# Expert weights loaded in two parts from two copied tables, in a two-layer decoder on one Trainium2 core

## The chip, the core and the metric

One core of a Trainium2 chip runs the whole program. The time is in device microseconds (us) for one execution; lower is better. The engines are PE (TensorE: matrix products and transposes; PEld is its weight load), DVE (VectorE), ACT (ScalarE), POOL (GpSimd) and SP (SyncE, which here only issues DMAs). Each engine works through its own instructions in a fixed order. Sixteen DMA engines are shared by all queues: q1 takes what SP issues, q0 what POOL issues, q10 what ACT issues.

## The reference

Sixteen blocks of 128 tokens, 512 wide, go through two decoder layers, each of self attention, cross attention and a feed-forward part, with a layernorm after each of the six. The first attention of layer 0, where a part of the change ends up, is

```
scores = einsum('btkgd,bskd->bkgts', qg, k) * scale + tril(ones)
p = softmax(scores, axis=-1)
out = einsum('bkgts,bskd->btkgd', p, v).reshape(B, T, C) @ wo.T + bo
```

The last part of layer 1, which the change is about, is a mixture of experts. A gate picks 2 of 8 experts for each of the 2048 tokens; each expert has a gate and an up weight (512 x 352 each) and a down weight (352 x 512), and a shared expert of twice that width serves all tokens:

```
logits = x @ gate_weight.T; scores = softmax(logits)
topk_w, topk_idx = top_k(scores, 2)
gu = einsum('th,efh->tef', x, gate_up_weights)
act = silu(gu[..., :F]) * gu[..., F:]
y = einsum('tef,te,ehf->th', act, combine, down_weights)
y += (silu(x @ sg.T) * (x @ su.T)) @ shared_down.T
```

All of it is in float32.

## The kernel before

**The stages** follow each other on PE nearly without a break: first attention (to about 260 us), cross attention of layer 0, its ternary feed-forward part (from about 743 us; called FFN below), linear attention, cross attention of layer 1, and the experts (from about 1489 us). A scheduler orders the instructions of each engine when the program is built. It keeps dependences and whatever is marked `keep_in_program_order`; anything else it may put elsewhere in its engine's queue.

**The first attention** works block by block. For each block and each of four groups of heads (a chunk, below), PE makes scores (L488), DVE adds the mask and takes the maximum (L212, L214), ACT takes the exponentials with their sums (L219), DVE the reciprocal of the sums (L225), and POOL scales the probabilities by it (`finish`, L226). One block later PE transposes the probabilities (`turn`, L231) and multiplies them with the values (L494). Beside this, the products of the next four blocks (L165) are dealt out between the chunks. POOL also prepares rotated weights (L377) and adds an output bias to the 16 blocks of x (L448, 1.26 us each). Between 12 and 61 us SP's queue brings in x, copies of x for later (`turned<-in_x`, L393, from DRAM to DRAM in pieces of 128 bytes), and two raw weight blocks of 1728 KB (L424).

**The experts.** The two choices of each token are ranked and sorted into 39 tiles of 128 token places (`NT`), each tile of one expert. For each tile a row list `which` tells which 128 rows of the weight array to fetch. A tile's weights (`ew`) are 128 partitions x 4352 floats, 2.23 MB: the first 2816 columns (`GU`) are gate and up, the last 1536 the down weights. There are three buffers for them (`HELD`). One indirect DMA, issued by POOL (`Tile.load`, L1241), fills a buffer from the input array `l1f_w`. Tile t uses buffer t modulo 3. Where tile t has the same expert as tile t - 3, the row numbers are set out of bounds and the DMA moves nothing, so an expert costs at most three real loads.

The loop over steps (from 1657 us on) is a pipeline. In step s: tile s is transposed by DVE (`turn`); `up` (L1271) makes gate and up of tile s - 1; `turn_act` (L1283) and `down` (L1292) finish tile s - 2; then a share of the shared expert's down products (L1326, L1334) follows on PE. The load for tile s + 1 is issued after the down products of tile s - 2, the last readers of that buffer. After it POOL issues the accumulating DMA that adds the tile's result to the DRAM array `sums` (L1304). That one waits for the accumulation before it, so POOL's queue in a step reads: load, accumulate. The token rows come through SP's queue in pieces of 512 bytes (`xs<-slots_x`, L1253).

After the last tile, `sums` is read back and the last layernorm ends the program (to 2057.5 us).

Of the kernel before, what the change touches and what calls it, by code (L numbers as in the profile page):

```python
# [12 lines left out]
F32 = mybir.dt.float32  # L13
# [33 lines left out]
def decoder_kernel(ctx: ExitStack, tc: tile.TileContext, a: dict, out: bass.AP):  # L47
# [669 lines left out]
    p2w.__exit__(None, None, None)  # L717
    psum.share(mm=2, sc=3, pt=2, av=1)

    wq4 = []
    with tc.tile_pool(name="p3", bufs=1) as p3:
        w1, w2 = (tern.w[n].rearrange("p (k f) -> p k f", k=KC) for n in range(2))
        def inputs(g):
            xh = p3.tile([P, KC, TG], F32R, tag="xh", name="xh", bufs=2)
            xl = p3.tile([P, KC, TG], F32R, tag="xl", name="xl", bufs=2)

            turns = [Turn(g * GB + i) for i in range(GB)]  # L730

            def sent(i):
                turns[i].send(p3)
                turns[i].fetch(p3, bufs=2)

            def one(i):
                at = slice(i * P, (i + 1) * P)
                if g == 0:
                    tr = bank(("mm", "sc")[i % 2], [P, KC, P], "tr")
                    for k in range(KC):  # L740
                        nc.tensor.transpose(tr[:, k, :], x[i][:, k * P : (k + 1) * P], ident)
                else:
                    tr = p3.tile([P, KC, P], F32, tag="xT", name="xT")
                    turns[i].back(tr)
                nc.scalar.copy(xh[:, :, at], tr)
                nc.vector.tensor_tensor(xl[:, :, at], tr, xh[:, :, at], ALU.subtract)

            if g == 0:
                return (xh, xl), [lambda i=i: one(i) for i in range(GB)]
            order = [(sent, 0), (sent, 1), (one, 0), (sent, 2), (one, 1), (sent, 3), (one, 2), (None, 0), (one, 3)]  # L750
            return (xh, xl), [lambda f=f, i=i: f and f(i) for f, i in order]

        xs, todo = inputs(0)
        for run in todo:
            run()
        todo = [lambda q=q: tern.cut(2, q, p3, tern.load(2, q, p3)) for q in range(NP)]
        todo.pop(0)()
        todo.pop(0)()
        for g in range(NG):
            hs = []  # L760
            if g + 1 < NG:
                coming, more = inputs(g + 1)
                todo += more
            for f in range(NF0):
                for _ in range(-(-len(todo) // (NF0 - f)) if f else 0):
                    todo.pop(0)()
                pa = bank("sc", [P, TG], "pa")
                pb = bank("pt", [P, TG], "pb")
                for dst, wt in ((pa, w1), (pb, w2)):
                    for k in range(KC):  # L770
                        for n in range(2):
                            nc.tensor.matmul(  # L772
                                dst, lhsT=wt[:, k, f * P : (f + 1) * P], rhs=xs[n][:, k, :],
                                start=(k == 0 and n == 0), stop=(k == KC - 1 and n == 1),
                            )
                sg = p3.tile([P, TG], F32, tag="sg", name="sg", bufs=2)
                nc.scalar.activation(sg, pa, AF.Sigmoid)
                ht = p3.tile([P, TG], F32, tag="ht", name="ht", bufs=2)
                nc.vector.tensor_tensor(ht, sg, pb, ALU.mult)
                hh = p3.tile([P, TG], F32R, tag="hh", name="hh", bufs=NF0 + 1)  # L780
                nc.scalar.copy(hh, ht)  # L781
                hl = p3.tile([P, TG], F32R, tag="hl", name="hl", bufs=NF0 + 1)
                nc.gpsimd.tensor_tensor(hl, ht, hh, ALU.subtract)  # L783
                hs.append((hh, hl))
            w3 = tern.w[2].rearrange("p (f d) -> p f d", d=D)
            if g + 1 < NG:
                xs = coming
            else:

                for n in range(2):  # L790
                    t = pre.tile([P, 2, 3 * D], F32, tag="pre", name=f"wq4{n}")
                    nc.sync.dma_start(t, a["l1a_wqkv"][:, 2 * n : 2 * n + 2, :])
                    wq4.append(t)
            for i in range(GB):
                b = g * GB + i
                po = bank("mm", [P, D], "po")
                for f in range(NF0):
                    for n in range(2):
                        nc.tensor.matmul(  # L799
                            po, lhsT=hs[f][n][:, i * P : (i + 1) * P], rhs=w3[:, f, :],  # L800
                            start=(f == 0 and n == 0), stop=(f == NF0 - 1 and n == 1),
                        )
                nc.vector.tensor_tensor(x[b], x[b], po, ALU.add)
                layernorm(b)
# [245 lines left out]

    GU = KC * 2 * FE
    with tc.tile_pool(name="p6", bufs=1, reuse_waits="tile") as p6:
        acts, halves = {}, {}
        w12 = []
# [167 lines left out]
                    ))  # L1224


        table = a["l1f_w"].rearrange("n p f -> (n p) f")
        with tc.tile_pool(name="p6r", bufs=1, side="right", reuse_waits="tile") as p6r:

            held = []  # L1230
# [1 line left out]
            class Tile:  # L1232
                def __init__(self, t):
                    self.t = t

                def load(self):
                    t = self.t
                    if t < HELD:
                        held.append(p6.tile([P, EW], F32, tag="ew", name=f"ew{t}", bufs=HELD))
                    self.w = held[t % HELD]  # L1240
                    tc.keep_in_program_order(nc.gpsimd.indirect_dma_start(  # L1241
                        out=self.w, out_offset=None, in_=table,
                        in_offset=bass.IndirectOffsetOnAxis(ap=which[:, t : t + 1], axis=0),
                        bounds_check=E * P - 1, oob_is_err=False,
                    ))
# [16 lines left out]
                        self.x.rearrange("p t (k a) -> p t k a", k=KC),  # L1262
                    ))

                def up(self):
                    gu = gate_up(self.w)
                    pg = bank("sc", [P, FE], "rg")
                    pu = bank("sc", [P, FE], "ru")
                    for dst, off in ((pg, 0), (pu, FE)):
                        for k in range(KC):  # L1270
                            nc.tensor.matmul(  # L1271
                                dst, lhsT=self.xT[:, k, :], rhs=gu[:, k, off : off + FE],
                                start=(k == 0), stop=(k == KC - 1),
                            )
                    sg = p6.tile([P, FE], F32, tag="sg", name="rsg", bufs=3)
                    nc.scalar.activation(sg, pg, AF.Silu)  # L1276
                    self.act = p6r.tile([P, FE], F32, tag="ract", name="ract", bufs=2)
                    nc.vector.tensor_tensor(self.act, sg, pu, ALU.mult)
# [9 lines left out]
                def down(self, following):  # L1288
                    dn = down_w(self.w)
                    po = bank("av", [P, D], "ry")  # L1290
                    for m_, mw in enumerate(ECH):
                        nc.tensor.matmul(  # L1292
                            po, lhsT=self.actT[:mw, m_, :], rhs=dn[:mw, m_, :], start=(m_ == 0), stop=(m_ == 2)
                        )
                    if following is not None:
                        following.load()
                    place = p6r.tile([P, 1], mybir.dt.int32, tag="place", name="place", bufs=3)
                    own = NC + NB + self.t
                    tc.keep_in_program_order(
                        nc.vector.tensor_tensor(place, self.told[:, 1:2], ramp[:, own : own + 1], ALU.add)  # L1300
                    )
                    y = p6.tile([P, D], F32, tag="y", name="ry", bufs=3)
                    nc.vector.tensor_scalar(y, po, self.told[:, 0:1], None, ALU.mult)
                    nc.gpsimd.indirect_dma_start(  # L1304
                        out=sums, out_offset=bass.IndirectOffsetOnAxis(ap=place, axis=0),
                        in_=y, in_offset=None, compute_op=ALU.add,
                    )
# [39 lines left out]
            for g in range(NG):  # L1347
                for n in range(2):
                    if (n, g) != (0, 0):
                        hidden(n, g, send)  # L1350
                if g != 2:
                    ahead[len(ahead)] = Tile(len(ahead))
                    ahead[len(ahead) - 1].load()
            for t in ahead.values():
                t.fetch()

# [5 lines left out]
            for step in range(NT + 2):  # L1362
# [5 lines left out]
                if step < NT:  # L1368
                    ahead[step].turn()
                if 0 <= step - 1 < NT:  # L1370
                    ahead[step - 1].up()
                if 0 <= step - 2:
                    ahead.pop(step - 2).down(ahead[step + 1] if step + 1 < NT else None)
                if step < NT:
# [189 lines left out]
```

## Time and profile before

| What | Time, us |
|---|---|
| runs of the kernel before | 2058.14, 2063.01, 2064.41 (median 2063.01) |
| the profiled execution, its own time | 2059.38 |
| its span, first to last instruction | 2057.5 |
| PE busy in the span | 2006.5 |
| POOL busy in the span | 647.5 |
| 39 weight loads on POOL (L1241), in all | 40.6 |
| 39 accumulating issues on POOL (L1304), in all | 61.8 |

The profile is of one execution. A "busy" time counts an engine's own instructions; the clock granted to PE was 0.992 of full speed over the span. In a row of the timeline the columns are start, duration, engine, line, operation, output<-inputs, shape and how many equal instructions were merged; a bracket at the end tells how long the engine was idle just before, and what ended that. In a row of the waits they are: who waited, for whom, microseconds in total, how many times, the longest. In a table by windows each row is one stretch of the span, with the busy time of each engine, the granted clock, the busy share of the DMA engines and the bytes they moved in GB/s.

### The profile page before, as it was taken

Reading aid. Unit: us, or ns where it says so; the run is one execution under the profiler, and the core shown is the slowest. Engines: PE = TensorE matmul, PEld = TensorE weight load, DVE = VectorE, ACT = ScalarE, POOL = GpSimd, SP = SyncE. Lnnn points to the kernel's source line nnn. Section 1 sums busy time; section 2 is a strip of 40 time slices with the busy share of each in tenths; the row PEclk is TensorE's granted clock in tenths of the full one; section 3 lists DMA queues with packets and bytes.
Section 4 is the critical chain, followed back from the end, with each engine's and each line's share of the span. In section 5 each row is a group of like instructions: output and inputs, shape, how many; then the busy total and the mean of one; then the engine's idle time right before and its main releaser. Section 6 shows DMA issues by size and latency. Waiting matters only on the chain.

```text
span 2057.5 us, 25359 instructions
## 1 busy us (share of the span) xinstructions
PE 2006.5 (98%) x9045; PEld 1110.9 (54%) x9045; DVE 886.6 (43%) x1775; ACT 627.7 (31%) x2107; POOL 647.5 (31%) x674
## 2 busy tenths in 40 slices
PE   8999999999999999999999999999899999999997
PEld 4555554444444468888554444555544455555552
DVE  4777732445554354342134414777731123233234
ACT  3555532333333333222311012766522200000002
POOL 7445520211222122223422113455613212323223
PEclk9999999999999999999999999999999999999999
DMA  9201241535432241001410018500013246786844
GB/s 250 87 17 40 104 143 56 158 118 174 149 124 91 71 121 60 16 11 62 147 42 21 11 41 265 203 22 22 27 61 116 95 133 185 226 247 192 264 89 169
DMA packets 164110, 227.87 MB, mean 111 GB/s; under 512 B 50576, under 2 KB 117520, under 8 KB 159248
## 3 DMA queue, kind: packets, MB, share of 16 engines
q1 hardware_dynamic: 149088, 152.80, 23.9%
q0 software_dynamic: 13792, 72.14, 11.6%
q8 instruction: 72, 1.18, 0.2%
q10 hardware_dynamic: 1104, 1.31, 0.2%
q14 instruction: 54, 0.44, 0.1%
HBM read 185.88 MB, written 75.83 MB: 127 GB/s over the span
## 4 chain that ended last, share of the span: by engine, by line
PE 84%; DMA 6%; DVE 3%; POOL 2%; issue 2%; ACT 1%; SPq 0%; POOLq 0%; DVEq 0%; ACTq 0%
PE po L649 10%; PE po L176 7%; PE pq L590 5%; PE pq L868 5%; PE pq L165 5%; PE pg L1143 4%; PE po L799 4%; PE pa L772 4%; PE pb L772 4%; PE pu L1143 3%; DMA sums<-ry,place 3%; PE ry L1292 3%; PE rg L1271 3%; PE ru L1271 3%; PE pv L878 3%; PE av L637 3%
## 5 line engine op out<-in xcount | busy, mean ns | idle before, releaser
L226 POOL TENSOR_TENSOR p<-p,rs 128x512 f32<-128x512 f32 x192 | 201.0, 1048 | 456.9 <-DVE rs L225 447.6
L649 PE MATMUL po<-mT,cc 128*128 128x512 f32 x512 | 230.4, 598 | 1.4 <-ACT cc L642 1.4
L219 ACT ACTIVATE p<-t,nmx 128x128 f32<-128x128 f32 x512 | 198.6, 390 | 33.8 <-POOL p L226 10.2
L649 PEld LDWEIGHTS po<-mT,cc 128*128 128x128 f32 x512 | 94.7, 190 | 115.0 <-issue 106.0
L219 ACT ACTIVATE p<-sc,nmx 128x128 f32<-128x128 f32 x256 | 90.3, 374 | 109.1 <-DVE nmx L214 93.8
L1241 POOL DMA_INDIRECT ew<-in_l1f_w_dram,which x39 | 40.6, 1042 | 246.6 <-PE ry L1292 167.2
L176 PE MATMUL po<-wo,oT 128*128 128x512 f32 x256 | 116.9, 600 | 0.4 <-ACT qkT L454 0.4
L590 PE MATMUL pq<-xT,wqr 128*128 128x512 f32 x256 | 115.8, 593 | 0.9 <-ACT xT L129 0.9
L1276 ACT ACTIVATE rsg<-rg 128x352 f32<-128x352 f32 x39 | 18.1, 464 | 320.6 <-PE rg L1271 297.0
L115 POOL TENSOR_SCALAR ve<-mv 128x1 f32<-128x1 f32 x80 | 17.8, 223 | 301.4 <-DVE mv L113 282.9
L868 PE MATMUL pq<-xT,wq 128*128 128x512 f32 x256 | 110.6, 592 | 0.7 <-ACT xT L129 0.7
L1292 PE MATMUL ry<-ew,ractT 128*128 128x512 f32 (+1 forms) x234 | 106.9, 592 | 0.0
L1271 PE MATMUL rg<-ew,xsT 128*128 128x352 f32 x312 | 100.1, 463 | 6.6 <-DMA ew<-in_l1f_w_dram,which 6.5
L122 POOL TENSOR_SCALAR x<-x,mv,rstd 128x512 f32<-128x512 f32 x48 | 100.5, 2094 | 4.5
L1271 PE MATMUL ru<-ew,xsT 128*128 128x352 f32 x312 | 98.7, 459 | 0.0
L219 ACT ACTIVATION_READ_ACCUMULATOR p<-t,nmx 128x1 f32 x512 | 96.3, 188 | 0.0
L233 DVE COPY pT<-pt 128x512 f32<-128x512 f32 x128 | 86.6, 679 | 19.4 <-PE pt L231 19.4
L783 POOL TENSOR_TENSOR hl<-ht,hh 128x512 fp32r<-128x512 f32 x44 | 57.4, 1305 | 108.1 <-ACT hh L781 108.1
L231 PEld LDWEIGHTS pt<-ident,p 128*128 128x128 f32 x512 | 60.6, 143 | 55.5 <-issue 41.5
L1143 PE MATMUL pg<-xT,sw_gu 128*128 128x512 f32 x192 | 86.5, 593 | 0.0
L1304 POOL DMA_INDIRECT sums<-ry,place x39 | 61.8, 1585 | 70.4 <-DMA sums<-ry,place 34.7
L214 DVE TENSOR_REDUCE nmx<-t 128x4 f32<-128x512 f32 x128 | 83.6, 676 | 0.8
(243 smaller groups left out, 3612.4 us busy)
## 6 DMA issues: line engine op xcount, KB each, us to landing
piece<-in_l0f_w_dram SPq DMA_DIRECT2D x48, 352.0 KB
away<-sq SPq DMA_DIRECT2D x32, 512.0 KB
pT<-away SPq DMA_DIRECT2D x128, 128.0 KB
raw<-in_l0x_raw_dram SPq DMA_DIRECT2D x8, 1728.0 KB
x<-turned SPq DMA_DIRECT2D x176, 64.0 KB
slots_x<-zero SPq DMA_DIRECT2D x1, 10023.0 KB
sums<-zero SPq DMA_DIRECT2D x1, 9984.0 KB
xs<-slots_x SPq DMA_DIRECT2D x156, 64.0 KB
```

Source lines behind the costliest of these rows:

```text
L122: engine.tensor_scalar(x[b], x[b], mean, rstd, ALU.subtract, ALU.mult)
L165: nc.tensor.matmul(got["p"], lhsT=lhsT, rhs=rhs, start=(n == 0), stop=(n == len(pairs) - 1))
L176: nc.tensor.matmul(po, lhsT=oT[:, c, :], rhs=wo[:, c, :], start=(c == 0), stop=(c == KC - 1))
L219: nc.scalar.activation(self.p[:, j, :], src[:, j, :], AF.Exp, bias=nmx[:, j : j + 1], accum_out=self.sm[:, j : j + 1])
L226: nc.gpsimd.tensor_tensor(self.p, self.p, spread(rs, P), ALU.mult)
L590: nc.tensor.matmul(pq, lhsT=wqr[:, k, cols], rhs=xT[:, k, :], start=(k == 0), stop=(k == KC - 1))
L649: nc.tensor.matmul(self.po, lhsT=self.cc[:, 4 * par + j, :], rhs=mT[h], start=(par == 0 and j == 0), stop=(par == 1 and j == 3),)
L772: nc.tensor.matmul(dst, lhsT=wt[:, k, f * P : (f + 1) * P], rhs=xs[n][:, k, :], start=(k == 0 and n == 0), stop=(k == KC - 1 and n == 1),)
L868: nc.tensor.matmul(pq, lhsT=wq4[k // 2][:, k % 2, c * P : (c + 1) * P], rhs=xT[:, k, :], start=(k == 0), stop=(k == KC - 1))
L1143: nc.tensor.matmul(dst, lhsT=sw_gu[:, k, at : at + P], rhs=xTs[g][:, k, :], start=(k == 0), stop=(k == KC - 1),)
L1271: nc.tensor.matmul(dst, lhsT=self.xT[:, k, :], rhs=gu[:, k, off : off + FE], start=(k == 0), stop=(k == KC - 1),)
L1292: nc.tensor.matmul(po, lhsT=self.actT[:mw, m_, :], rhs=dn[:mw, m_, :], start=(m_ == 0), stop=(m_ == 2))
```

## The change

Two DRAM arrays, `tables[0]` (8 x 128 rows of 2816 floats) and `tables[1]` (8 x 128 rows of 1536), are made, and the experts' weights are copied into them from `l1f_w`: sixteen copies from DRAM to DRAM, issued by POOL, written into the task list of the FFN, and not marked `keep_in_program_order`. `Tile.load(n)` then fetches one part of the weights from `tables[n]` into its columns of the buffer. The gate and up part of tile s + 2 is issued in step s after the gate and up products of tile s - 1, and the down part of tile s + 1 after the down products of tile s - 2. So each tile has two indirect DMAs in place of one, 78 in all.

```
+    GU = KC * 2 * FE
+    tables = [dram.tile([E * P, w], F32, tag=f"table{n}", name=f"table{n}") for n, w in enumerate((GU, EW - GU))]
...
+        def part_weights(e, n):
+            part = (slice(0, GU), slice(GU, EW))[n]
+            nc.gpsimd.dma_start(tables[n][e * P : (e + 1) * P, :], a["l1f_w"][e, :, part])
...
             if g + 1 < NG:
                 coming, more = inputs(g + 1)
                 todo += more
+            if g > 0:
+                for m_, e in enumerate(range(3 * g - 3, min(3 * g, E))):
+                    for n in range(2):
+                        todo.insert(min(3 * m_ + n, len(todo)), lambda e=e, n=n: part_weights(e, n))
...
-        table = a["l1f_w"].rearrange("n p f -> (n p) f")
...
-                def load(self):
+                def load(self, n):
...
-                    if t < HELD:
+                    if t < HELD and n == 0:
                         held.append(p6.tile([P, EW], F32, tag="ew", name=f"ew{t}", bufs=HELD))
                     self.w = held[t % HELD]
+                    part = (slice(0, GU), slice(GU, EW))[n]
                     tc.keep_in_program_order(nc.gpsimd.indirect_dma_start(
-                        out=self.w, out_offset=None, in_=table,
+                        out=self.w[:, part], out_offset=None, in_=tables[n],
...
-                def up(self):
+                def up(self, following):
...
+                    if following is not None:
+                        following.load(0)
...
                     if following is not None:
-                        following.load()
+                        following.load(1)
...
-                    ahead[len(ahead) - 1].load()
+                    ahead[len(ahead) - 1].load(0)
+                    ahead[len(ahead) - 1].load(1)
...
-                    ahead[step - 1].up()
+                    ahead[step - 1].up(ahead.get(step + 2) if step > 0 else None)
```

More of the change, by code (lines that the diff above doesn't have):

```diff
@@ L1047, in decoder_kernel @@
     p5w.__exit__(None, None, None)
-    GU = KC * 2 * FE
     with tc.tile_pool(name="p6", bufs=1, reuse_waits="tile") as p6:
```

## The prediction, made before the changed kernel was run

> **What bounds the kernel now.** I read the page's sums first, then the table by windows for the stages, then PE's waits and its timeline inside the expert loop.
>
> ```profile
> span 2057.5 us, 25359 instructions
> PE 2006.5 (98%) x9045; PEld 1110.9 (54%) x9045; DVE 886.6 (43%) x1775; ACT 627.7 (31%) x2107; POOL 647.5 (31%) x674
> ```
> ```profile
> core 0: us, PE busy (x) PEld busy (x) DVE busy (x) ACT busy (x) POOL busy (x), PEclk, DMA share, GB/s
> 0.00:60.00 60.00, 50.48 (x250) 30.39 (x254) 26.87 (x43) 23.68 (x81) 39.76 (x42) 0.97 0.88 249
> 60.00:1657.00 1597.00, 1575.20 (x7637) 874.44 (x7635) 733.09 (x1434) 573.79 (x1971) 491.14 (x531) 0.99 0.26 85
> 1657.00:2004.00 347.00, 340.41 (x1073) 190.24 (x1072) 104.32 (x242) 18.11 (x39) 97.52 (x74) 1.00 0.70 198
> ```
>
> PE is the bound nearly everywhere. In the expert loop, the stage that the change is about, only 347.0 - 340.4 = 6.6 us of 347 are free of PE work. So however well the loads go, little can be won there. PE's waits in that window have one row, and the timeline shows what one of those waits does:
>
> ```profile
> PE rg L1271 <- DMA ew<-in_l1f_w_dram,which: 6.5, 8, 1.6
> ```
> ```profile
> 1761.31 2.53 PE L1271 MATMUL ru<-ew,xsT 128*128 128x352 f32 x8
> 1763.68 2.74 PE L1292 MATMUL ry<-ew,ractT 128*128 128x512 f32 x6
> 1766.26 1.02 PE L1326 MATMUL po<-sw_dn,act 128*128 128x512 f32 x2
> 1767.12 0.49 PE L1283 MATMUL rt<-ident,ract 128*128 128x128 f32 x3
> 1768.63 2.63 PE L1271 MATMUL rg<-ew,xsT 128*128 128x352 f32 x8 [1.02 <-DMA ew<-in_l1f_w_dram,which]
> ```
>
> In the chain of waits such a product counts 2.63 us where an unhindered one counts 2.37: it starts cold, without overlap. So the eight waits cost 6.5 + 8 x 0.26 = 8.6 us. That is the whole prize of the split.
>
> **The loads (part one, on the path).** Before, the load for this tile went out on POOL at 1757.33, after the down products, and landed at about 1768.6: 11.25 us by the chain, against a step of 8.50 us (1741.05 to 1749.55). Now the gate and up part, 2816 / 4352 of the bytes, goes out one product group after `up` of the tile three before; to its use are three steps less one `up` (4.7 us), 3 x 8.5 - 4.7 = 20.8 us. The down part keeps its place but is needed only at `down`, one step and more later than before. Both leads are over the 11.25 us that the whole load took, so I remove all eight waits: -8.6. What is late next would be the DMA engines: 2.23 MB at the 399 GB/s of 1752 to 1756 is 5.6 us of a step, and POOL's three issues in a step (1.03 + 1.03 + 1.59 us and three gaps of 0.3, 4.6 us of 8.5) also fit. So the bound of this gain is -8.6 at best and 0 at worst, if the accumulations, which wait for each other on POOL (34.7 us in all), hold the earlier issue back. I take -8.6, since the new lead is nearly twice the time that the load took.
>
> **The copies (part two).** By the diff they lie beside the FFN. The order of the built instructions says otherwise: nothing holds the copies there, and the scheduler has put all sixteen at the front of POOL's queue in the first attention. Seven stand before the first scaling of probabilities (L226), among L377 and L448; the other nine among the scalings of the first three blocks. PE's and SP's orders are the same in both kernels; on DVE and ACT a few neighbours change places. What POOL does there now:
>
> ```profile
> 15.17 4.08 POOL L377 TENSOR_TENSOR t<-w,rsn 128x256 f32<-128x256 f32 x4 [0.63 <-DVE wr L381]
> 19.21 1.26 POOL L448 TENSOR_TENSOR x<-x,bo 128x512 f32<-128x512 f32 x1
> 20.43 2.31 POOL L377 TENSOR_TENSOR t<-w,rsn 128x256 f32<-128x256 f32 x2
> 22.71 18.86 POOL L448 TENSOR_TENSOR x<-x,bo 128x512 f32<-128x512 f32 x15
> 41.53 2.04 POOL L226 TENSOR_TENSOR p<-p,rs 128x512 f32<-128x512 f32 x2
> ```
> ```profile
> 42.62 0.69 PE L231 MATMUL pt<-ident,p 128*128 128x128 f32 x2 [0.61 <-POOL p L226]
> 43.10 6.48 PE L165 MATMUL pq<-xT,wr 128*128 128x512 f32 x12
> 49.42 0.38 PE L231 MATMUL pt<-ident,p 128*128 128x128 f32 x2
> ```
>
> POOL is full from 15.17 to 43.57 and PE already waits 0.61 us for its first scaling. So what seven issues take from POOL goes straight to PE, and PE's later work moves with it, since no later stage has a wait that would absorb it. A direct DMA issued by POOL is not in this trace. From below: the shortest issue on SP, 0.30 us (`x<-turned`); from above: POOL's accumulating issue, 1.59 us and a gap of 0.3. The nearest row is POOL's plain indirect issue of 128 rows:
>
> ```profile
> 1540.25 0.98 POOL L1221 DMA_INDIRECT slots_x<-row,slot  x1 [0.49 <-issue]
> 1541.54 0.96 POOL L1221 DMA_INDIRECT slots_x<-row,slot  x1 [0.31 <-issue]
> ```
>
> One starts 1.29 us after the other. I take 1.3: 7 x 1.3 = 9.1, less the 0.63 us that POOL idles before 15.17, is +8.5. The bounds are 7 x 0.3 - 0.6 = +1.5 and 7 x 1.9 - 0.6 = +12.7. The other nine (12 us) lie beside PE: POOL is busy only 3.1 of the 10 us from 60 to 70, and of the second block's four scalings (first at 49.64) PE needs the first at 60.87, so there is a cover of some 10 us. If it were gone, they would cost up to 12 more.
>
> The bytes of the copies: 8 x 2.23 = 17.8 MB, in a stretch where the DMA engines are busy to 0.88. Eight copies move up to about 51 us (8.9 MB, 22 us at 399 GB/s), so SP's transfers that end at 61 end by about 83. The first raw block is needed at 85.9 and the turned x at 87.3, both moved by the 8.5 us as well. I cost it at nothing; without this cover it would cost what it is late, some us.
>
> The rest is nothing: three more issues before the loop lie beside the shared products; the changed neighbours on DVE and ACT in the FFN are needed a group later.
>
> **Sum.** -8.6 + 8.5 = -0.1 us: 2059.3 against the profiled execution's 2059.4. That one stood 3.6 us below the median of 2063.0; on the median's footing it is 2062.9. I forecast 2062. A measurement of this kernel tells about 0.3% (6.2 us) from no change.
>
> **Rivals.**
> *Cheap issues, faster.* If a direct issue on POOL costs as little as SP's (0.3 us), the copies cost 1.5 and the prize stays: 2059.4 - 8.6 + 1.5 = 2052, or 2056 on the median's footing, -7.1. For it speaks that a direct DMA has no row list to read; against it that all issues on POOL, load or store, take 0.96 to 1.6 us.
>
> *A lane held, slower.* In the built order the ninth copy waits for the first to have landed, the tenth for the second, and so on: the sixteenth waits on POOL, at about 83 us, for the eighth, issued at about 51, and behind it stand the scalings that PE needs some 6 us later. It decides if the five copies issued from 40 to 51 us (5.24 MB) have not landed by 89, below 5.24 MB / 49 us = 107 GB/s. The only DRAM to DRAM copies in the trace run at 132 GB/s in all, in 128-byte pieces:
>
> ```profile
> DMA packets 5059, 0.66 MB, mean 132 GB/s; under 512 B 5058, under 2 KB 5058, under 8 KB 5058
> ```
>
> Were the new ones as slow and had to share with SP's queue by half, 66 GB/s, they would land at 119: +30, about 2093. Against it: their rows are 6 to 11 KB, and x in 2 KB rows came in at 392 GB/s (16 to 24 us). The Trainium skill, "DMA: Bandwidth & Descriptors", section "Anatomy of one DMA", fits a DMA issued by GpSimd as 2.0 us plus bytes over 436 GB/s; by that (an estimate from that page) the five would take 22 us one after the other and the lane would be free long before. The same page in "Issuing engine by pattern" gives plain copies to Sync, not to GpSimd, which speaks against this change, as POOL's row above does.
>
> *The waits stay, slower.* If the accumulations or the DMA engines still end last, the loop wins 0 to 1 and the copies' 8.5 remain: +7.5, about 2070. It decides if the split load still lands later than 20.8 us after its issue.
>
> A rule on the issue cost is in "SBUF — State Buffer" of the Trainium skill, in the box on DVE blocking DMA: a GpSimd-issued DMA of 0.62 us took 3.1 us beside a DVE copy in its two-port mode. By that, seven issues would cost 21 us; DVE's rows from 15 to 42 us are two-input products and reductions, and no such copy stands there.
>
> **Numbers.** Cancelling, within 0.3%: 0.62. Cheap issues: 0.13, faster. The waits stay: 0.12; a lane held: 0.08; issues dearer than 1.9 us: 0.05; these three slower, 0.25. The range goes from the cheap issues on the profiled footing, 2052, to the case of the waits that stay with an issue cost between 1.3 and 1.9 us, 2073, and leaves out the lane.
>
> **What would show it.** POOL's timeline with seven direct issues of about 1.3 us before a first L226 at about 50 us, and PE's wait before its first L231 grown from 0.61 to about 9 us. In the expert loop no wait of PE on `ew`, and a window of about 338 us in place of 347. It is wrong if POOL shows a long wait on a DMA between 60 and 90 us, if the direct issues are far from 1.3 us, or if L1271 still waits for `ew`.

## The result, and the profile after

| | before | after |
|---|---|---|
| median of 7 runs each, us | 2063.01 (2058.14 to 2064.67) | 2071.21 (2069.85 to 2072.25) |
| the profiled execution | 2059.38 | 2071.26 |
| its span | 2057.5 | 2069.3 |
| first gate product of the expert loop (`rg`) | 1657.8 | 1679.2 |
| last down product of the loop (`ry`) | 2003.2 | 2015.1 |

The change makes the kernel slower: ratio 1.0041, 95% interval 1.0031 to 1.005, or +8.2 us on the medians. The forecast was no change, 2062 us.

The last two rows give the start of each product, and they split the difference at once. PE comes to the expert loop 21.4 us late, and the loop then takes 335.9 us instead of 345.4, so it gives 9.5 us back. The loop did what was predicted. What was not predicted is at the front.

The page of the changed kernel. PE's busy time is up by 1.0 us and the span by 11.8, so nearly all of the loss is waiting. q0 is what POOL issues; it had 13792 packets and 72.14 MB before.

```profile
span 2069.3 us, 25502 instructions
...
PE 2007.5 (97%) x9045; PEld 1112.7 (54%) x9045; DVE 886.4 (43%) x1775; ACT 627.7 (30%) x2107; POOL 695.4 (34%) x729
...
q1 hardware_dynamic: 149088, 152.80, 23.9%
q0 software_dynamic: 21712, 89.97, 14.5%
```

The table by windows of the changed kernel (columns as in the prediction: PE's busy time is first after the length, PEclk is third from the end). It answers where the waiting is. In 94 to 108 us PE works 4.04 of 14 us, where before it was busy 13.97; in 40 to 50 its clock is at half. The expert loop, last row, is full: 337.00 of 337.00, where before 340.41 of 347. The second fence has three of these stretches in the kernel before: from 50 to 86 us its DMA engines were busy to 0.19, now to 0.96.

```profile
40.00:50.00 10.00, 6.23 (x15) 3.77 (x16) 4.80 (x10) 4.77 (x24) 9.70 (x11) 0.50 1.00 317
50.00:86.00 36.00, 35.58 (x210) 20.05 (x208) 21.16 (x44) 21.52 (x92) 16.92 (x21) 1.00 0.96 315
86.00:94.00 8.00, 3.79 (x46) 1.69 (x44) 5.21 (x11) 4.04 (x19) 4.78 (x5) 1.00 0.97 147
94.00:108.00 14.00, 4.04 (x18) 2.58 (x19) 1.74 (x4) 0.45 (x1) 1.04 (x1) 0.52 0.81 239
...
1679.00:2016.00 337.00, 337.00 (x1072) 189.94 (x1072) 103.81 (x241) 18.06 (x39) 134.68 (x111) 1.00 0.74 203
```
```profile
40.00:50.00 10.00, 9.16 (x35) 4.98 (x32) 6.39 (x15) 7.35 (x35) 6.00 (x7) 0.83 1.02 297
50.00:86.00 36.00, 35.58 (x246) 20.18 (x246) 24.41 (x51) 21.94 (x95) 15.52 (x17) 1.00 0.19 62
...
94.00:108.00 14.00, 13.97 (x86) 7.96 (x86) 10.08 (x23) 8.01 (x35) 7.72 (x8) 1.00 0.48 164
```

PE's waits over the whole span of the changed kernel (who waited, for whom, total, times, longest). No row names `ew` any more. The row on top is new; the wait for the first scaled probabilities (L226) was 0.6 before.

```profile
PE pc L311 <- DMA raw<-in_l0x_raw_dram: 14.2, 1, 14.2
...
PE pt L231 <- POOL p L226: 4.2, 3, 3.8
```

The chain of waits of the changed kernel from 0 to 130 us (start, length, what). SP's issuing of the `turned` copies (L393) is 48.6% of it; two of the eight issues take 27 and 20 us. Only when they are done does SP issue the raw block, and PE begins on it at 103.96.

```profile
by line: SPq L393 48.6%; DMA x<-in_x_dram 9.3%; DMA raw<-in_l0x_raw_dram 7.7%; DMA w<-in_l0a_wqkv_dram 6.4%; PE po L176 5.3%; PE pq L165 4.7%; PE pt L231 2.7%; SPq L95 2.4%; PE pm L325 2.4%; PE pg L332 1.5%; PE sc L488 1.5%; SPq L398 1.3%; 
...
39.12 27.07 SPq L393
66.23 20.30 SPq L393
...
93.88 10.04 DMA raw<-in_l0x_raw_dram
103.96 1.55 PE pc L311 x12
```

SP's timeline, before the change and then after it (start, length, queue, line). The same eight issues take 14.80 us and then 64.04, and the raw block behind them goes out at 40.94 and then at 93.88.

```profile
23.53 14.80 SPq L393 DMA_DIRECT2D turned<-in_x_dram  x8
...
40.94 0.34 SPq L424 DMA_DIRECT2D raw<-in_l0x_raw_dram  x1
```
```profile
27.09 64.04 SPq L393 DMA_DIRECT2D turned<-in_x_dram  x8
...
93.88 0.34 SPq L424 DMA_DIRECT2D raw<-in_l0x_raw_dram  x1
```

The DMA queues of the changed kernel in the window 48 to 52 us (queue: packets, MB, share of the 16 engines). POOL's queue and SP's passed the same number of packets, 157 each. One side's are about 8 KB, the other's 128 bytes: 1.30 MB against 0.02. SP's pieces hold 3.2% of the engines' time and get no more.

```profile
DMA packets 314, 1.32 MB, mean 330 GB/s; under 512 B 173, under 2 KB 173, under 8 KB 229
...
q0 software_dynamic: 157, 1.30, 94.9%
q1 hardware_dynamic: 157, 0.02, 3.2%
```

Most of the windows of 4 us from 44 to 80 us look alike (179 of SP's to 178 of POOL's from 52 to 56, 128 to 128 from 56 to 60), but not all: from 60 to 64 it is 390 to 188, from 64 to 68 271 to 147. In the whole of 44 to 80 us 1809 of SP's pieces pass beside 1438 of POOL's packets. Outside it the counts are far from equal, though the copies run there too: 1505 to 116 from 32 to 36, 1408 to 121 from 80 to 84. The counts are sums over sixteen engines, and no run shows whether both queues had work on each of them then. After 88 us, with the copies done, SP's pieces pass at 5183 in 4 us.

POOL's timeline of the changed kernel: seven direct issues stand before the first scaling, as the order of the instructions had said, but one takes 0.54 us, the very first 0.81.

```profile
14.36 0.81 POOL L759 DMA_DIRECT2D table<-in_l1f_w_dram  x1
...
26.68 0.58 POOL L759 DMA_DIRECT2D table<-in_l1f_w_dram  x1
...
30.92 0.54 POOL L759 DMA_DIRECT2D table<-in_l1f_w_dram  x1
...
37.61 1.55 POOL L759 DMA_DIRECT2D table<-in_l1f_w_dram  x3
...
40.38 0.54 POOL L759 DMA_DIRECT2D table<-in_l1f_w_dram  x1
40.93 3.70 POOL L448 TENSOR_TENSOR x<-x,bo 128x512 f32<-128x512 f32 x3
44.60 1.03 POOL L226 TENSOR_TENSOR p<-p,rs 128x512 f32<-128x512 f32 x1
```

### The profile page after: what moved, and what is told of

It reads as the page before. It is cut to its first block, busy times and chain, and to the rows that moved or that the text cites. A ratio compares the mean times of both kernels' runs of the same rounds, so it can differ in the third digit from the quotient of the medians.

```text
span 2069.3 us, 25502 instructions
## 1 busy us (share of the span) xinstructions
PE 2007.5 (97%) x9045; PEld 1112.7 (54%) x9045; DVE 886.4 (43%) x1775; ACT 627.7 (30%) x2107; POOL 695.4 (34%) x729
## 3 DMA queue, kind: packets, MB, share of 16 engines
q0 software_dynamic: 21712, 89.97, 14.5%
## 4 chain that ended last, share of the span: by engine, by line
PE 88%; SPq 3%; DVE 3%; DMA 2%; ACT 1%; POOL 1%; issue 1%; POOLq 0%; DVEq 0%; ACTq 0%
PE po L649 10%; PE po L176 7%; PE pq L590 5%; PE pq L880 5%; PE ry L1306 5%; PE rg L1283 4%; PE ru L1283 4%; PE pq L165 4%; PE pg L1154 4%; PE po L811 4%; PE pa L784 4%; PE pb L784 4%; PE pu L1154 3%; SPq L393 3%; PE pv L890 3%; PE av L637 3%
## 5 line engine op out<-in xcount | busy, mean ns | idle before, releaser
L226 POOL TENSOR_TENSOR p<-p,rs 128x512 f32<-128x512 f32 x192 | 200.9, 1047 | 468.9 <-DVE rs L225 460.9
L1253 POOL DMA_INDIRECT ew<-table,which x78 | 79.4, 1018 | 236.6 <-PE ru L1283 111.2
L115 POOL TENSOR_SCALAR ve<-mv 128x1 f32<-128x1 f32 x80 | 17.8, 223 | 303.7 <-DVE mv L113 285.2
L176 PE MATMUL po<-wo,oT 128*128 128x512 f32 x256 | 116.8, 600 | 0.4 <-ACT qkT L454 0.4
L1290 ACT ACTIVATE rsg<-rg 128x352 f32<-128x352 f32 x39 | 18.1, 463 | 311.2 <-PE rg L1283 304.0
L795 POOL TENSOR_TENSOR hl<-ht,hh 128x512 fp32r<-128x512 f32 x44 | 57.3, 1302 | 108.2 <-ACT hh L793 108.2
L231 PEld LDWEIGHTS pt<-ident,p 128*128 128x128 f32 x512 | 60.5, 142 | 59.5 <-issue 42.3
L231 PE MATMUL pt<-ident,p 128*128 128x128 f32 x512 | 79.2, 279 | 5.1 <-POOL p L226 4.2
```

Of the source, the lines that this page charges most:

```text
L176: nc.tensor.matmul(po, lhsT=oT[:, c, :], rhs=wo[:, c, :], start=(c == 0), stop=(c == KC - 1))
L226: nc.gpsimd.tensor_tensor(self.p, self.p, spread(rs, P), ALU.mult)
L231: nc.tensor.transpose(pt[:, j, :], self.p[:, j, :], ident)
```

## The experiments

The theory, called T1 below: SP's 128-byte pieces and POOL's big packets share the DMA engines about packet for packet, so the copies, hoisted into the first attention, stretch SP's L393 from 15 to 64 us; raw, issued behind them, comes 14 us late. The rivals: the issues on POOL are the cost; or the bytes of the copies fill the DMA engines and delay raw whatever the packets are; or the split loads themselves cost something later.

**Tables given.** The two tables come laid out as inputs, so there are no copies; the loads are split as in the change.

```
-    tables = [dram.tile([E * P, w], F32, tag=f"table{n}", name=f"table{n}") for n, w in enumerate((GU, EW - GU))]
+    tables = [a[f"l1f_t{n}"].rearrange("n p f -> (n p) f") for n in range(2)]
...
-                        todo.insert(min(3 * m_ + n, len(todo)), lambda e=e, n=n: part_weights(e, n))
```

> The split alone: the two tables are laid out by the host as inputs, and no copy runs. Theory (the split is worth the eight waits in the expert loop, and all of the loss is in the copies at the start): no wait of PE on ew, the loop as short as in the changed kernel (337 us from 1657.8 on), the start as before, so about 9 us less than before, near 2054. Rival (something in the split itself costs, such as the 39 more issues on POOL or a longer end): less than 4 us gained, 2059 or more.

Measured 2049.49 us, ratio 0.9938 (0.9924 to 0.9951) to the kernel before, 12.6 us faster. The first gate product is at 1658.9 us and the loop takes 335.9, the same as in the changed kernel. So the split loads cost nothing and bring even more than the 8.6 that the prediction had for them (and more than the 9 expected of this run); all that the change loses is due to the copies.

**Copies only.** The kernel before with the sixteen copies added where the change has them; nothing reads the tables and the loads are the old ones.

```
+    tables = [dram.tile([E * P, w], F32, tag=f"table{n}", name=f"table{n}") for n, w in enumerate((GU, EW - GU))]
...
+                        todo.insert(min(3 * m_ + n, len(todo)), lambda e=e, n=n: part_weights(e, n))
```

> The copies alone: the kernel before with the sixteen copies, whose tables nobody reads. Theory (the copies hold SP's queue at the start, so that PE waits 14 us for the first raw block, 3 us for its first scaled probabilities and some 3 us more at half clock): about 20 us more than before, 2083, with the long wait of PE on raw near 90 us. Rival (the copies cost 12 and the split brings nothing): 2075.

Measured 2079.48 us, ratio 1.0088 (1.007 to 1.0106), +17.4. PE's waits of this kernel: the one for raw is there whole, the old one for `ew` too (in this kernel `rg` is at L1282).

```profile
PE pc L311 <- DMA raw<-in_l0x_raw_dram: 14.7, 1, 14.7
...
PE rg L1282 <- DMA ew<-in_l1f_w_dram,which: 6.8, 7, 2.1
...
PE pt L231 <- POOL p L226: 4.2, 2, 3.9
```

The first gate product is at 1678.1, 20.3 us late, as in the changed kernel (21.4). The time, 2079.5, lies between the 2083 expected and the rival's 2075; the waits, and the tables given, decide for the theory. The two halves of the change thus add up: -12.6 + 17.4 = +4.8, against the +8.2 measured; the intervals of the three ratios are 4 to 7 us wide, so the difference of 3.4 does not call for a third effect.

**Issues only.** As copies only, but each copy moves 16 columns: all sixteen issues, hardly any bytes.

```
-            nc.gpsimd.dma_start(tables[n][e * P : (e + 1) * P, :], a["l1f_w"][e, :, part])
+            nc.gpsimd.dma_start(tables[n][e * P : (e + 1) * P, 0:16], a["l1f_w"][e, :, part.start : part.start + 16])
```

> The kernel before with sixteen copies of 16 columns in place of the whole width: POOL issues as many DMAs at the start, but they move 0.13 MB in place of 17.8. Theory (the bytes on the DMA engines are the loss, the issues cost what seven to fourteen of them take from POOL, 0.54 us each): PE's wait for its first scaled probabilities 4 to 8 us, no wait on raw, 2067 to 2071. Rival (the issues on POOL are the loss): 2075 or more.

Measured 2068.82 us, ratio 1.0026 (1.0016 to 1.0037), +6.8. Here all sixteen issues stand before the first scaling, at 0.52 us each (8.6 us by POOL's timeline), where the change has seven. So this run is the cost of sixteen issues on the path, not of seven: the first gate product is at 1665.7, 7.9 us late. PE's waits of this kernel:

```profile
PE rg L1282 <- DMA ew<-in_l1f_w_dram,which: 10.7, 12, 1.9
...
PE pt L231 <- POOL p L226: 7.4, 2, 7.2
```

There is no wait for raw, SP's L393 takes 15.18 us, and raw goes out at 41.23. The issues alone do not make it late: it is what the copies move. The row for `rg` shows something else: with the old loads, this execution waited 10.7 us in twelve places, the profiled one of before 6.5 in eight.

**Pinned.** The changed kernel with one edit, which holds the copies where they are written, in the task list of the FFN.

```
-            nc.gpsimd.dma_start(tables[n][e * P : (e + 1) * P, :], a["l1f_w"][e, :, part])
+            tc.keep_in_program_order(nc.gpsimd.dma_start(tables[n][e * P : (e + 1) * P, :], a["l1f_w"][e, :, part]))
```

> The changed kernel with its copies kept in program order, so that they really are issued beside the FFN. Theory (the loss comes from where the copies fall, on SP's 128-byte pieces that the first attention waits for): no wait of PE on raw, the loop 337 us, 2054 to 2058. Rival (17.8 MB cost their time wherever they are moved, since SP's transfers in the FFN then wait as long): PE waits in the FFN, 2065 or more.

Measured 2050.01 us, ratio 0.9941 (0.9928 to 0.9955): 12.1 us faster than before, and faster than the 2054 to 2058 expected. POOL's timeline of this kernel shows the issues between POOL's split of the hidden rows (L795), in time that POOL had free:

```profile
812.31 1.28 POOL L795 TENSOR_TENSOR hl<-ht,hh 128x512 fp32r<-128x512 f32 x1 [2.54 <-ACT hh L793]
813.54 1.40 POOL L759 DMA_DIRECT2D table<-in_l1f_w_dram  x2
816.00 1.28 POOL L795 TENSOR_TENSOR hl<-ht,hh 128x512 fp32r<-128x512 f32 x1 [1.06 <-ACT hh L793]
817.24 0.53 POOL L759 DMA_DIRECT2D table<-in_l1f_w_dram  x1
```

and the table by windows that the front is as it was before: PE 50.56 of the first 60 us (before 50.48), and the DMA engines at 0.18 from 60 to 110.

```profile
0.00:60.00 60.00, 50.56 (x250) 30.37 (x250) 26.84 (x42) 23.67 (x81) 39.75 (x42) 0.97 0.90 250
60.00:110.00 50.00, 49.55 (x316) 28.19 (x313) 39.74 (x83) 31.07 (x137) 24.74 (x26) 1.00 0.18 58
1657.00:1994.00 337.00, 337.00 (x1072) 189.94 (x1071) 104.26 (x241) 18.07 (x39) 135.32 (x111) 1.00 0.74 203
```

With its 17.8 MB and its sixteen issues in the program, the front costs nothing, and the time is that of the tables given. Beside the FFN the DMA engines had room: from 813 to 946 us their share goes from 0.04 before to 0.44, and PE is busy for all of the 133 us in both kernels. So neither the bytes nor the issues are dear as such; their place is. This kernel is faster than the kernel before and than the changed one.

**Raw first.** The changed kernel with the first two raw loads ahead of the `turned` copies in SP's queue.

```
...
+        raws = []
+        for i in range(2):
+            raws.append(rawp_.tile([P, 2, RAW], F32, tag="raw", name=f"raw{i}"))
+            nc.sync.dma_start(raws[i], a["l0x_raw"][i].rearrange("p (h n) -> p h n", h=2))
         for g in range(2, NG):
...
```

> The changed kernel, with SP's first two raw loads put ahead of the eight copies of x (`turned`, L393) in its queue; the expert copies stay at the front of POOL's queue. Theory (SP's 128-byte pieces are held up by the big packets of the expert copies, and raw is only late because it stands behind them): raw is issued before 30 us and lands by about 45, PE's wait of 14.2 us for raw is gone, but the copies of x still take 50 to 65 us on SP, so that the turned x, needed at about 87 to 90 us, comes last in its place: a new wait of 5 to 12 us some microseconds later. Time between 2062 and 2071, against 2071 for the change. Rival (the bytes alone fill the DMA engines, whatever the packets): raw, 3.5 MB more ahead of everything, delays x or the expert copies by 9 us, and the copies of x take about their 15 us plus that; no wait over 5 us on the turned x, time near 2056.

Measured 2071.2 us, ratio 1.0041 (1.0028 to 1.0055): the same as the change. SP's timeline and then PE's waits of this kernel (its lines are numbered a little higher: the `turned` copies are L399; the output projection L176 waits for DVE, and DVE's next x, L154, waited 14.55 us for `x<-turned`):

```profile
26.91 0.95 SPq L395 DMA_DIRECT2D raw<-in_l0x_raw_dram  x2
28.13 70.29 SPq L399 DMA_DIRECT2D turned<-in_x_dram  x8
```
```profile
PE po L176 <- DVE cT L315: 14.5, 1, 14.5
...
PE pt L231 <- POOL p L226: 4.0, 2, 3.8
```

The wait for raw is gone, and the turned x comes last in its place. The expectation had this wait at 5 to 12 us and the copies at 50 to 65; they are 14.5 and 70, and the time is just above its 2062 to 2071. The rival, by which the copies of x would take about their 15 us, is out. Raw was late only because of what stood before it. The DMA queues of this kernel from 44 to 80 us pass their packets one for one in sum:

```profile
q0 software_dynamic: 1505, 11.63, 94.7%
q1 hardware_dynamic: 1504, 0.21, 3.6%
```

**Whole rows.** The changed kernel with the turned x made by eight copies on ACT and stored from SBUF in rows of 2 KB, 1024 packets in place of 16384 from DRAM to DRAM. The same bytes land, and the expert copies stay hoisted.

```
-                nc.sync.dma_start(
-                    turned[blocks].rearrange("n p (q k a) -> (n p) q k a", q=4, k=KC)[:, :, k, :],
-                    a["x"][blocks].rearrange("n p (k q a) -> (n p) k q a", q=4, k=KC)[:, k],
-                )
...
+            nc.scalar.copy(
+                tmp[:, n].rearrange("p (q k a) -> p q k a", q=4, k=KC), x[b].rearrange("p (k q a) -> p q k a", k=KC, q=4)
+            )
+            nc.sync.dma_start(turned[b], tmp[:, n])
```

> The changed kernel, with the turned x of blocks 8 to 15 made by eight copies on ACT and stored by SP in rows of 2 KB, in place of the DRAM to DRAM copies in pieces of 128 bytes; the same bytes land, 1024 packets instead of 16384. The expert copies stay where the change has them. Theory (packets are shared one for one between SP's queue and POOL's, so a queue of small packets is starved): SP's part no longer lasts 64 us, raw is issued by about 60 us and PE's wait for it goes from 14.2 us to under 4; with the issue cost of about 3 us and a little clock left, 2054 to 2060. Rival (what delays raw is the 17.8 MB that the copies move): the bytes are the same, raw still lands at about 100 us, PE's wait stays at 10 to 14 us and the time at 2067 to 2072.

Measured 2057.02 us, ratio 0.9972 (0.9962 to 0.9982). SP's timeline of this kernel: 8 us for the stores, and raw out at 41.16.

```profile
28.39 7.97 SPq L399 DMA_DIRECT2D turned<-tmp  x8
...
41.16 0.72 SPq L425 DMA_DIRECT2D raw<-in_l0x_raw_dram  x1
```

Its DMA queues from 48 to 52 us again pass 178 packets each, but here SP's carry more (in the whole of 44 to 80 us 1325 and 1326 packets, 2.51 MB of SP's):

```profile
q0 software_dynamic: 178, 1.23, 84.8%
q1 hardware_dynamic: 178, 0.14, 11.7%
```

PE does not wait for raw at all, though the same copies run beside these stores and the DMA engines are busy to 1.00 from 50 to 86 us. That goes against "the bytes". What this kernel still loses is of its own making: its copies on ACT stand before the first products' evictions, PE waits 5.8 us for `qkT`, and the first gate product is at 1664.7, 6.9 us late. The run changes where the turned x comes from as well as its pieces, so by itself it does not tell packet size from origin; for the size speak the equal packet counts.

**Finer rows.** The changed kernel with the gate and up copies cut into rows of 2848 bytes, so that more big packets pass and, by T1, more small ones with them.

```
...
-            nc.gpsimd.dma_start(tables[n][e * P : (e + 1) * P, :], a["l1f_w"][e, :, part])
+            to, src = tables[n][e * P : (e + 1) * P, :], a["l1f_w"][e, :, part]
+            if n == 0:
+                to = to.rearrange("p (k f) -> p k f", k=KC)
+                src = bass.AP(src.tensor, src.offset, [[EW, P], [2 * FE, KC], [1, 2 * FE + 8]])
+            nc.gpsimd.dma_start(to, src)
...
```

> The changed kernel, with the eight copies of gate and up cut into rows of 2848 bytes (four to a row of the table, which is padded by 32 bytes a piece) in place of rows of 11264 bytes; the bytes rise by 1 per cent of these, the packets of the sixteen copies from 2048 to 5120. Theory (one small packet of SP's queue passes for each packet of POOL's): some 3000 more of the 16384 small packets pass while the copies run, at some 1000 packets in a microsecond when they are alone that is 3 us: SP's part of 64 us shrinks by 2 to 6 us, PE's wait for raw from 14.2 to 9 to 12 us, time 2066 to 2070, if POOL's issues do not grow. Rival (bytes): nothing shrinks, 2071. A third outcome, issues on POOL that grow with the number of rows: PE's wait before its first L231 goes above 4 us and eats the gain.

Measured 2071.19 us, ratio 1.0037 (1.0025 to 1.005). The expectation failed: L393 takes 64.55 us, and PE waits 15.6 for raw. One step of it did not come about: the rows did not become packets of 2848 bytes. POOL's queue has 22736 packets in all, 1024 more than the change and not 3072; the copies are 3328 of them (2304 in the change), of 5.4 KB in the mean. The third outcome came about in part: an issue of these copies takes 0.72 us in the median instead of 0.54, but PE's wait at its first L231 is 3.0 us, not above 4. Of the 16384 small pieces 1000 more could pass, which is 1 us at their rate alone, and the copies were no faster for it (303 against 330 GB/s, both queues together, from 48 to 52 us). The time thus tells nothing between the theories. The packets do: the window 48 to 52 us of this kernel has again the same count in both queues, at a different size.

```profile
DMA packets 435, 1.21 MB, mean 303 GB/s; under 512 B 234, under 2 KB 234, under 8 KB 435
...
q0 software_dynamic: 218, 1.19, 93.0%
q1 hardware_dynamic: 217, 0.03, 4.7%
```

From 44 to 80 us SP passed 2144 packets here to 2065 of POOL's; in the other two kernels 1504 to 1505 and 1325 to 1326, and in the changed kernel itself 1809 to 1438. In that stretch POOL's big packets set the pace, and SP's follow about one for one. Why far more of SP's pass at other times, and in two windows of the changed kernel, stays open.

## Why the prediction was wrong, step by step

- **The failed step: the bytes of the copies.** "SP's transfers that end at 61 end by about 83 ... I cost it at nothing". The step divided bytes by 399 GB/s, as if only their sum counted. What counted was packets: from 44 to 80 us, 36 of the 64 us that L393 took, 1809 of its 16384 pieces of 128 bytes passed beside 1438 of POOL's packets, 50 and 40 in a microsecond; with the copies done SP's pass at about 1300 in one. So L393 ended at 91 and raw left at 93.88 instead of 40.94. PE's wait: 14.2 us, in place of nothing. The prediction had even read the row with 5058 pieces under 512 bytes, but used it for the speed of the new copies, not for what these would do to the old ones. Two runs show the step: issues without bytes make no wait for raw, and whole rows beside the same bytes make none either.
- The step was also short in its own terms: it counted the bytes of eight copies and left the other eight out. POOL's queue had moved 7.64 of the 17.83 MB by 52 us; the rest went on to 88. By the same division all of them are 45 us, which puts the end of SP's transfers at 106 and past the 94 at which, by the prediction, raw was needed (85.9 and the 8.5 of the issues). A late raw forecast from that sum would have been right by luck: the whole rows run has the same bytes and no wait for raw.
- The Trainium skill states the rule in "DMA: Bandwidth & Descriptors", section "Queues, rings and completion order": a DMA engine goes round between the queues that it has work for, and changes over at packet boundaries. The counts from 44 to 80 us agree with it (1504 to 1505 with raw first), if what the profile counts as a packet is what the page calls one, which no run here shows. What it costs a queue of small packets is this case's own number: 64 us for what took 15.
- **The issues on the path**, +8.5, came to +3.2 (PE's wait at its first L231, from 0.61 to 3.77). The place and the number, seven, were right; a direct issue is 0.54 us, not 1.3. The nearest row, an indirect issue, was the wrong neighbour; SP's 0.30, the lower bound, was nearer. The other nine cost nothing beside PE, as predicted: L231 waits 0.4 us more in all.
- **The clock.** Nothing in the sum stood for it. Around its longer waits PE ran at half clock: for 10.2 us from 39.9 (before: 3.4 us from 42.0), and for 13.7 us from 94.5, of which PE worked the last 4.2. PE's shift against before goes from 3.85 us at 64 to 18.1 at raw and 19.9 at 112, so by this difference the two cost an estimated 0.7 and 1.8 beyond the waits themselves; later stages add 1.5 to the 21.4, part of it at a third such stretch at 313 us (13.7 us, before 10.2).
- **The loads**, -8.6, were right in mechanism: no wait on `ew`, a full window of 337. In size the profile gave -9.5. On medians it was more: the two kernels that have the split loads and no loss at the front are 12.1 and 12.6 us faster. The old loop is the reason that can be seen: it took 345.4, 347.2 and 350.4 us in the three profiled executions with the old loads (before, copies only, issues only), and 335.9 in each of the six with the new. The profiled execution of before had the shortest of the three, and stood 3.6 below its median; the prediction noted that, and took it for footing only. That the prize is larger in the median execution than in this one is an inference from these three; the loop of the other executions is not on record.
- **The rivals.** No lane was held: POOL has no long wait on a DMA between 60 and 90 us. The waits did not stay; that this rival had 2070 and 2071 was measured is luck. Cheap issues were half true: 0.54 us is near that rival's price, and with the copies out of the way the time, 2050, is faster than its 2052 to 2056. The result fell on the slower side by a mechanism that no rival had: a stalled queue of SP in front of raw.

Sum of the profiled executions: 3.2 + 14.2 + 4.0 (clock and small shifts) = 21.4 late at the loop, -9.5 in it, -0.1 after it: 11.8, the difference of the spans. On medians, 21.4 - 12.1 = 9.3 against the 8.2 measured. Left open is why the stretch from the last down product to the end differs from execution to execution (49.8 to 54.3 us in the nine profiles, whatever the kernel); one profile's span should not be read finer than that.

## What to carry to other kernels

When a transfer is added beside others, count packets per queue, not only bytes: a queue of small pieces can be slowed to about one piece per packet of the other queue, as here from 44 to 80 us, and everything behind it in the same issuing queue waits too, needed first or not. A bulk copy without a consumer nearby has no reason to stay where it is written, so pin it to a stretch whose DMA engines are idle: one marker made the difference between 0.4% slower and 0.6% faster. Where bytes are divided by a rate, count all that move in the stretch, not only those of the first issues. And take the prize of a removed wait from several executions where the wait is a race that is lost by a microsecond or two.

## What the runs showed of the hardware beyond that

- Two queues on the DMA engines passed equal numbers of packets from 48 to 52 us in three kernels, at sizes of 8 KB against 128 bytes, 5.4 KB against 128 bytes, and 7 KB against some 0.8 KB.
- SP's issue of a DMA is not free when its queue is backed up: single issues of L393 lasted 27 and 20 us, and SP can issue nothing else meanwhile.
- A direct DMA issued by POOL took 0.52 to 0.65 us in the changed kernel, the first of the program 0.81, against 1.02 for an indirect one of the experts' loads (L1253, 78 of them). With the big rows cut in four the median was 0.72, the longest 1.04.
- Around PE's waits of 3 to 16 us between 28 and 110 us its granted clock was half, in stretches of 6.8, 10.2 or 13.7 us; with those of 3.4 that are also seen, all but the last of a program, which its end cuts off, are multiples of 3.4.
